# Group sums of the first image by TensorE, fewer loads, and layer 1's weights prepared in the opening

## The chip, the core and the metric

The kernel runs on one core of one Trainium2 chip, in one launch. The metric is the device time of that core in microseconds (us), taken from three runs; a further run was profiled, and the profile is what is read here. The core has TensorE (PE in the profile, its weight loads PEld), VectorE (DVE), ScalarE (ACT), GpSimd (POOL) and SyncE (SP), each with its own queue of instructions that runs in order. SP and ACT also issue the DMA transfers.

## The reference

Eight images of 384 channels and 32 x 32 tokens pass two layers of attention; layer 1 has a feed-forward part too. Cut to what matters here:

```python
x = x + _L0_conv_ref(_gn(x), L0_conv_qkv_w, ..., L0_conv_mlp_b2)
t = _to_tokens(x)
t = t + _L1_attn_ref(_ln_t(t), L1_attn_qkv_w, L1_attn_proj_w, L1_attn_proj_b)
t = t + _L1_ffn_ref(_ln_t(t), ...)

def _gn(v, G=32, eps=1e-5):                       # 32 groups of 12 channels
    g = v.reshape(B_, G, C_ // G, H_, W_)
    m = jnp.mean(g, axis=(2, 3, 4), keepdims=True)
    s = jnp.var(g, axis=(2, 3, 4), keepdims=True)
    return ((g - m) / jnp.sqrt(s + eps)).reshape(v.shape)

# in _L0_conv_ref: one bias table for all images, (heads, n, n), added to the scores
hidden = jax.nn.gelu(rel @ mlp_w1 + mlp_b1, approximate=False)
bias = hidden @ mlp_w2 + mlp_b2
return jnp.transpose(bias, (2, 0, 1))

# in _L1_attn_ref: q and k, per head of 64
def _normalize(t):
    mu = t.mean(axis=-1, keepdims=True)
    sd = t.std(axis=-1, keepdims=True, ddof=1)
    return (t - mu) / sd
```

In layer 1, subtracting the token's mean and the head's mean commutes with the projection, so the kernel takes both out of the weights once: from each column of the 384 x 1152 projection matrix its mean over the 384 channels, and from each row of a head's 64 columns their mean (for q and k).

## The kernel before, in words

All arithmetic is in 32-bit floats. Channels lie on the 128 partitions in KC = 3 chunks, tokens run along the free axis in two halves of 512. Layer 0 goes image by image: projections of q and k in pairs of heads (`project_qk`, L467, six groups named pq), of v (`project_v`, L495, four groups), then 32 units of scores and weighting. A unit computes scores for two heads (L521), adds the bias (L532, VectorE), takes the exponential (L536, ScalarE), and weighs v (L552) two units later. Four PSUM buffers of 128 x 1024 (`mm2`) serve everything. Layer 1 follows with the same shape and a feed-forward part behind.

The order on each engine is the order in which the program writes it; there is no planner. Work that is to stand beside other work is put into `later` with a number of steps: `later.step()` is called after each pq group, each v group and each unit, and runs what has come due. So in the first image steps 1 to 6 are the projections, 7 to 10 the v groups, and from 11 on the units.

The opening of the first image (L212 to L680) does this. The image is loaded in three chunks on SP; the raw weights of q and k (1.18 MB) are loaded into the space of `grow`, and `place_weights_qk` copies them on VectorE into the padded layout. Statistics of the channels (L418) are sent to DRAM and back on SP, so that the 12 channels of a group lie on one partition; there they are joined (L432), turned into scale and shift on GpSimd, and sent to DRAM and back again (L440, L444); then the image is normalised (L448).

The bias needs one value per head and relative position: 63 x 63 = 3969 of them (NREL). Positions are held in four row groups of 32 partitions, `hidden` computes the first MLP layer (L350) and Gelu (L355) in two rounds of four calls, and `table_part` the second layer (L370), writing its half of the table to DRAM on SP (L379). From the table, `grow_load` reads 32 parts (8 heads x 4), four DMAs of 117 KB each (L391), and `grow_turn` copies each part, turned, into `grow` (L401 on ScalarE, L403 on VectorE). 20 of the 32 parts are due before or at the first units, one per unit after that. The last twelve go through the space of `oT`. A part of the next head pair is used only some units later.

The other loads of layer 0 (bias of q and k in eight pieces, L311; weights of v, bias of v, output weights in six pieces, bias, L319 to L336) are issued by SP between the group norm and the table. ACT issues the small loads of the MLP (L238 to L246) before its first Gelu. [...]

Layer 1's weights are prepared in the last image of layer 0, by `_Start.stages`: loaded at unit 5, column sums by TensorE against a matrix of ones (L146, named cm) at units 10 and 12, their means subtracted by GpSimd (L158), and the heads' means (L164 to L166) at units 19, 21 and 23.

Of the kernel before, what the change touches and what calls it, by code (L numbers as in the profile page):

```python
# [27 lines left out]
P = 128  # L28
# [92 lines left out]
class _Start:  # L121
# [4 lines left out]
    def __init__(self, tc, ins, x1, shared):  # L126
        self.nc, self.ins, self.x1, self.shared = tc.nc, ins, x1, shared

    def load_weights(self):
        self.wqkv = self.shared.weights("wqkv").rearrange("p (k c) -> p k c", k=KC)  # L130
        self.nc.sync.dma_start(
            self.wqkv, self.ins["L1_attn_qkv_wT"].rearrange("(k p) c -> p k c", p=P)
        )
# [5 lines left out]
    def means(self, temp, at, n):  # L139
        nc = self.nc  # L140
        pm = self.shared.mm2(f"cm{at}")
        for h in range(-(-n // HALF)):
            w = min(HALF, n - h * HALF)
            for k in range(KC):
                cols = slice(at + h * HALF, at + h * HALF + w)
                nc.tensor.matmul(  # L146
                    pm[:, h, :w], self.shared.ones, self.wqkv[:, k, cols],
                    start=(k == 0), stop=(k == KC - 1),
                )
        self.mean = temp(f"cmean{at}")  # L150
        nc.scalar.activation(
            self.mean[:, :n], pm.rearrange("p h q -> p (h q)")[:, :n], AF.Copy, scale=1.0 / C
        )

    def subtract(self, at, n):
        for k in range(KC):
            w = self.wqkv[:, k, at : at + n]
            self.nc.gpsimd.tensor_sub(w, w, self.mean[:, :n])  # L158

    def heads(self, k):  # L160
        nc = self.nc
        w = self.wqkv[:, k, 0 : 2 * C].rearrange("p (h d) -> p h d", d=D1)
        hm = self.shared.pool.tile([P, 2 * H1], F32, tag="hm", name=f"hm{k}")
        nc.vector.tensor_reduce(hm, w, AX.X, ALU.add)  # L164
        nc.gpsimd.tensor_scalar(hm, hm, 1.0 / D1, 1.0, ALU.mult, ALU.mult)
        nc.gpsimd.tensor_sub(w, w, hm.unsqueeze(2).to_broadcast([P, 2 * H1, D1]))  # L166

    def stages(self, temp):

        first, rest = (0, 2 * HALF), (2 * HALF, 3 * C - 2 * HALF)  # L170
        return [
            (5, self.load_weights),
            (6, self.load_image),
            (10, lambda: self.means(temp, *first)),
            (11, lambda: self.subtract(*first)),
            (12, lambda: self.means(temp, *rest)),
            (14, lambda: self.subtract(*rest)),
            (19, lambda: self.heads(0)),
            (21, lambda: self.heads(1)),
            (23, lambda: self.heads(2)),  # L180
        ]


def _layer0(tc, ins, x1, sums, shared, beside):
# [9 lines left out]
    with ExitStack() as ctx:  # L194
# [31 lines left out]
        QT, QN = 32, 2 * HALF  # L226
# [5 lines left out]
        nc.vector.memset(rel, 0.0)  # L232
        nc.vector.memset(w2, 0.0)
        nc.vector.memset(b2, 0.0)
        for g in range(P // QT):
            at = g * QN
            n = min(QN, NREL - at)
            nc.scalar.dma_start(rel[g * QT : g * QT + 2, 0:n], ins["rel"][:, at : at + n])  # L238
            nc.scalar.dma_start(w1[g * QT : g * QT + 2], ins["L0_conv_mlp_w1"])
        with nc.allow_non_contiguous_dma(reason="a bias, once"):  # L240
            nc.scalar.dma_start(b1, ins["L0_conv_mlp_b1"].rearrange("(k p) -> p k", p=HC))
            nc.scalar.dma_start(
                w2[:, :, 0:H0], ins["L0_conv_mlp_w2"].rearrange("(k p) h -> p k h", p=HC)
            )
        for g in range(P // QT):
            nc.scalar.dma_start(b2[g * QT : g * QT + H0], ins["L0_conv_mlp_b2"].unsqueeze(1))  # L246
# [8 lines left out]
        first = load(0)  # L255

# [31 lines left out]

        def place_weights_qk():
            whole = 2 * NF0 * D0  # L290
            for s in range(2):
                nc.vector.tensor_copy(
                    wqk[:, :, s, :, 0:D0],
                    raw[:, :, s, 0:whole].rearrange("p k (h d) -> p k h d", d=D0),
                )
                for j in range(2):
                    at = whole + j * D0
                    nc.vector.tensor_copy(
                        wqk[:, :, s, j::2, D0:S0],
                        raw[:, :, s, at : at + D0].rearrange("p k (c d) -> p k c d", d=FR),  # L300
                    )

        def load_bias_qk():
            with nc.allow_non_contiguous_dma(reason="a bias, once"):
                for j in range(2):
                    for row, n, at, step in (
                        (j * S0, D0, j * D0, 2 * D0),
                        (j * S0 + D0, FR, (2 * NF0 + j) * D0, FR),
                    ):
                        for s in range(2):  # L310
                            nc.sync.dma_start(  # L311
                                bqk[row : row + n, s],
                                bass.AP(
                                    qkv_b.tensor, qkv_b.offset + s * C + at, [[1, n], [step, NF0]]
                                ),
                            )

        def load_weights_v_out():
            nc.sync.dma_start(wv, qkv_w[:, 2 * C : 3 * C].rearrange("(k p) c -> p k c", p=P))  # L319
            nc.sync.dma_start(bv, qkv_b[2 * C : 3 * C].partition_broadcast(P))  # L320
            pw = ins["L0_conv_proj_w"]
            for j in range(2):
                last = (2 * NF0 + j) * D0
                for row, n, at, step in (
                    (j * S0 + SP, D0, j * D0, 2 * D0),
                    (j * S0, FR, last, FR),
                ):
                    nc.sync.dma_start(
                        wp[row : row + n],
                        bass.AP(  # L330
                            pw.tensor, pw.offset + at * C, [[C, n], [step * C, NF0], [1, C]]
                        ),
                    )
                nc.sync.dma_start(wl[j * S0 + SP : (j + 1) * S0], pw[last : last + D0])
            with nc.allow_non_contiguous_dma(reason="a bias, once"):
                nc.sync.dma_start(bp, ins["L0_conv_proj_b"].rearrange("(k p) -> p k", p=P))  # L336
# [5 lines left out]
        def hidden(r):  # L342

            hids = {}
            for k in range(2):
                for a in range(2):
                    ph = mm2(f"ph{r}{k}{a}")
                    for i in range(2):
                        g = 2 * a + i
                        nc.tensor.matmul(  # L350
                            ph[0:HC, i], w1[g * QT : g * QT + 2, ts(k, HC)],
                            rel[g * QT : g * QT + 2, ts(r, HALF)], start=True, stop=True,
                        )
                    hid = etile(f"hid{r}{k}{a}", (HC, 2, HALF))
                    nc.scalar.activation(  # L355
                        hid.rearrange("p i q -> p (i q)"), ph[0:HC].rearrange("p i q -> p (i q)"),
                        AF.Gelu, bias=b1[:, k : k + 1],
                    )
                    hids[k, a] = hid
            return hids  # L360
# [5 lines left out]
        def table_part(r, hids):  # L366
            pb = mm2(f"pb{r}")
            for k in range(2):
                for g in range(P // QT):
                    nc.tensor.matmul(  # L370
                        pb[ts(g, QT), 0], w2[:, k, :], hids[k, g // 2][:, g % 2],
# [4 lines left out]
            for g in range(P // QT):  # L376
                at = g * QN + r * HALF
                n = min(HALF, NREL - at)
# [26 lines left out]
        def group_norm(b, xn):  # L405
# [48 lines left out]
            ]  # L454

# [184 lines left out]
        stages = group_norm(0, first)  # L640
        for stage in stages[:3]:
            stage()
        place_weights_qk()
        hids = [hidden(r) for r in range(2)]
        stages[3]()
        load_bias_qk()
        stages[4](nc.vector)
        load_weights_v_out()
        table_part(0, hids[0])
        later.after(1, lambda: table_part(1, hids[1]))  # L650
        nc.scalar.activation(tiny[:, 1:2], tiny[:, 0:1], AF.Exp)
# [14 lines left out]
        for i, n in enumerate((3, 3, 3, 3, 2, 2, 2, 2)):  # L666
            later.after(i + 3 + (i > 3), lambda n=n: grow_turns(n))
            later.after(i + 2, lambda n=n: grow_loads(n))
        for i in range(len(parts) - 20):
# [4 lines left out]
        with_last = beside(etile)  # L674
        for b in range(B):
            held = []
            for i, u in enumerate(units):
# [10 lines left out]
                if b == B - 1:  # L688
                    for at, work in with_last:
# [1085 lines left out]
def tile_conv_attn_hybrid(ctx: ExitStack, tc: tile.TileContext, ins, out):  # L1775
    dram = ctx.enter_context(tc.tile_pool(name="x1", bufs=1, space=DRAM))
    x1 = dram.tile([B, C, N], F32, tag="x1", name="x1")
    state = ctx.enter_context(tc.tile_pool(name="state", bufs=1))
    flag = state.tile([P, 1], mybir.dt.int32, tag="flag", name="flag")
    sums = state.tile([P, B, NP0, 2 * N // P], F32, tag="sums", name="sums")  # L1780
    with ExitStack() as main, tc.manual_schedule():
        shared = _Shared(tc, main)
        start = _Start(tc, ins, x1, shared)
        before = _layer0(tc, ins, x1, sums, shared, start.stages)
# [6 lines left out]
    with tc.If(out_of_range > 0):  # L1791
        _layer0_shifted(tc, ins, x1)
        with ExitStack() as again, tc.manual_schedule():
            shared = _Shared(tc, again)
            start = _Start(tc, ins, x1, shared)
            late = again.enter_context(tc.tile_pool(name="late", bufs=2))
            for _, stage in start.stages(
                lambda name: late.tile([P, N], F32, tag="t", name=name)
            ):
                stage()  # L1800
# [45 lines left out]
```

## Time and profile before

| | us |
|---|---|
| median of three runs (lowest, highest) | 3058.92 (3056.34, 3061.76) |
| the profiled execution, its own time | 3058.54 |
| its span, first to last instruction | 3056.7 |
| TensorE busy in the span | 3023.9 |
| VectorE, ScalarE, GpSimd busy | 1771.8, 1401.7, 463.0 |
| first TensorE matmul | 7.13 |
| first projection of layer 0 | 23.94 |
| first scores of layer 0 | 74.45 |
| first projection of the second image | 189.96 |
| first projection of layer 1 | 1440.39 |

The mean granted clock of TensorE is 0.998 of full. A row of the timeline or of the chain gives the start in us from the span's start, the duration in us, the engine, the line and what it writes and reads; "x16" is a count. TensorE's 32-bit matmuls appear as two records each, so a projection group of 6 matmuls is 12 records. A window's row gives busy time by engine, then the granted clock, the busy share of the 16 DMA engines and GB/s. The share of busy time is high for TensorE everywhere except in the first 100 us, where windows and timeline tell more than the page.

### The profile page before, as it was taken

How to read it: one execution, taken by the hardware profiler on the slowest of the kernel's cores; microseconds unless marked ns; L12 is line 12 of the kernel's file. 1: busy time of each engine (PE TensorE's matmuls, PEld its weight loads, DVE VectorE, ACT ScalarE, POOL GpSimd, SP SyncE). 2: the span in 40 equal slices, each digit the busy share in tenths (PEclk: the TensorE clock that was granted, in tenths of full speed). 3: DMA queues.
4: the chain of work that ended last, by engine and by line, in shares of the span. 5: the costliest groups of instructions: out<-in, count | busy, mean ns of one | idle time of the engine just before them, and what ended most of it. 6: DMA issues, size and time to landing. Idle time of an engine off the chain costs nothing.

```text
span 3056.7 us, 45678 instructions
## 1 busy us (share of the span) xinstructions
PE 3023.9 (99%) x18914; PEld 1595.5 (52%) x18914; DVE 1771.8 (58%) x1768; ACT 1401.7 (46%) x1768; POOL 463.0 (15%) x315
## 2 busy tenths in 40 slices
PE   8999999999999999999999999999999999999998
PEld 3455546455554646444545645645645645644443
DVE  3746647273655637355565765755765755755545
ACT  2634526252443616244453553553544543554544
POOL 0111102021110202123202202202202202211110
PEclk9999999999999999999999999999999999999999
DMA  7412020211202020222401101101101101102011
GB/s 178 118 26 83 19 82 23 71 30 26 76 22 79 23 85 17 50 74 60 117 23 30 50 23 30 50 23 30 50 22 30 50 22 30 50 16 71 16 51 44
DMA packets 102770, 150.49 MB, mean 49 GB/s; under 512 B 62260, under 2 KB 65828, under 8 KB 101784
## 3 DMA queue, kind: packets, MB, share of 16 engines
q1 hardware_dynamic: 99688, 147.41, 16.8%
q8 instruction: 152, 2.49, 0.3%
q14 instruction: 66, 0.54, 0.1%
q10 hardware_dynamic: 2864, 0.05, 0.1%
HBM read 111.05 MB, written 27.32 MB: 45 GB/s over the span
## 4 chain that ended last, share of the span: by engine, by line
PE 92%; DVE 3%; DMA 2%; ACT 1%; SPq 1%; issue 1%; ACTq 0%; DVEq 0%
PE o L552 15%; PE s L521 15%; PE s L1322 11%; PE o L1371 10%; PE pq L467 8%; PE pq L1178 7%; PE y2p L1572 5%; PE pp L616 4%; PE y1p L1521 4%; PE pp L1435 4%; PE pv L1259 4%; PE pv L495 4%; PE sum L1394 1%; DVE qk L1188 1%; PE hs L1207 1%
## 5 line engine op out<-in xcount | busy, mean ns | idle before, releaser
L536 ACT ACTIVATE e<-e 128x1024 f32<-128x1024 f32 x512 | 534.9, 1056 | 441.9 <-DVE e L532 425.3
L532 DVE TENSOR_TENSOR e<-s,grow 128x1024 f32<-128x1024 f32 x512 | 601.0, 1217 | 190.6 <-PE s L521 190.1
L521 PE MATMUL s<-qk 48*64 48x512 f32 x4096 | 605.8, 591 | 2.3 <-DVE e L532 2.2
L552 PE MATMUL o<-e,v 64*64 64x512 f32 x4096 | 603.4, 591 | 1.5 <-DVE e L532 1.5
L1333 ACT ACTIVATE e<-s,kc 128x512 f32<-128x512 f32 x768 | 463.3, 693 | 181.2 <-PE s L1322 164.5
L1322 PE MATMUL s<-qk,qk 64*64 64x512 f32 x3072 | 398.6, 592 | 0.6 <-DVE oT L1381 0.4
L1371 PE MATMUL o<-e,v 64*64 64x512 f32 x3072 | 395.5, 591 | 0.0
L521 PEld LDWEIGHTS s<-qk 48*64 48x64 f32 x4096 | 238.5, 132 | 226.6 <-issue 82.3
L552 PEld LDWEIGHTS o<-e,v 64*64 64x64 f32 x4096 | 257.9, 133 | 182.6 <-issue 80.9
L1348 DVE TENSOR_TENSOR t<-t,e 128x1024 f32<-128x1024 f32 x192 | 230.8, 1221 | 65.6 <-ACT e L1333 65.6
L1178 PE MATMUL pq<-bx,wqkv 128*128 128x512 f32 x576 | 255.4, 596 | 0.7 <-ACT tra L1150 0.7
L467 PE MATMUL pq<-xn,w 128*128 128x512 f32 x576 | 251.5, 597 | 0.0
L1322 PEld LDWEIGHTS s<-qk,qk 64*64 64x64 f32 x3072 | 148.7, 132 | 195.0 <-issue 116.2
L581 POOL TENSOR_TENSOR inv<-sums,over 128x16 f32<-128x16 f32 x32 | 92.7, 2898 | 1015.1 <-DMA sums<-sd 856.0
L1371 PEld LDWEIGHTS o<-e,v 64*64 64x64 f32 x3072 | 148.1, 133 | 180.7 <-issue 142.7
L467 PEld LDWEIGHTS pq<-xn,w 128*128 128x128 f32 x576 | 109.5, 191 | 142.7 <-issue 140.2
L1178 PEld LDWEIGHTS pq<-bx,wqkv 128*128 128x128 f32 x576 | 107.4, 190 | 145.3 <-issue 141.5
L1345 DVE TENSOR_TENSOR t<-e,e 128x1024 f32<-128x1024 f32 x96 | 114.1, 1224 | 62.7 <-ACT e L1333 62.7
L1194 ACT ACTIVATE qsq<-pq 128x1024 f32<-128x1024 f32 x48 | 49.1, 1023 | 215.4 <-DVE qk L1188 110.0
L1508 DVE TENSOR_REDUCE parts<-y 128x1 f32<-128x1024 f32 x75 | 90.0, 1217 | 94.9 <-ACT y L1505 94.4
L1228 POOL TENSOR_TENSOR hc<-hc,rsqrt 128x32 f32<-128x32 f32 x24 | 139.4, 5810 | 2.0
L477 DVE TENSOR_SCALAR qk<-pq,bqk 128x1024 f32<-128x1024 f32 x24 | 30.8, 1284 | 177.6 <-PE pq L467 177.6
(161 smaller groups left out, 3028.3 us busy)
## 6 DMA issues: line engine op xcount, KB each, us to landing
rb<-rd SPq DMA_DIRECT2D x112, 256.0 KB
xn<-in_x_dram SPq DMA_DIRECT2D x24, 512.0 KB
res<-in_x_dram SPq DMA_DIRECT2D x24, 512.0 KB
x<-res SPq DMA_DIRECT2D x24, 512.0 KB
bx<-x SPq DMA_DIRECT2D x8, 1536.0 KB
rq<-hi SPq DMA_DIRECT2D x48, 256.0 KB
out_dram<-bx SPq DMA_DIRECT2D x24, 512.0 KB
wide<-table SPq DMA_DIRECT2D x80, 114.2 KB
```

What stands on the lines that cost most here:

```text
L467: nc.tensor.matmul(pq[:, h], wqk[:, k, s, 2 * pair : 2 * pair + 2, :].rearrange("p h d -> p (h d)"), xn[:, k, ts(h, HALF)], start=(k == 0) ...
L521: nc.tensor.matmul(s[j][ts(c, QP), i], qk[pair][rows, 1, ts(4 * m2 + 2 * i + c, QP)], qk[pair][rows, 0, ts(h, HALF)], start=True, stop=True,)
L532: nc.vector.tensor_add(e.rearrange("p (i q) -> p i q", i=2), s[j], bass.AP(near.tensor, near.offset, [near.ap[0], [-QROWS * IW, 2], [1, HA ...
L536: nc.scalar.activation(e, e, AF.Exp)
L552: nc.tensor.matmul(po[ts(j, S0), r], v[keys, 2 * m2 + i, 2 * pair + j, :], es[j][keys, ts(i, HALF)], start=(m2 == 0 and i == 0), stop=(m2 ...
L1178: nc.tensor.matmul(pq[:, h], wqkv[:, k, s * C + pair * P : s * C + (pair + 1) * P], xt[:, k, ts(h, HALF)], start=(k == 0), stop=(k == KC - 1),
L1228: nc.gpsimd.tensor_tensor(c, c, rsqrt.to_broadcast(list(c.shape)), ALU.pow)
L1322: nc.tensor.matmul(s[j][ts(c, QP), i], qk[pair, 1][rows, ts(4 * m2 + 2 * i + c, QP)], qk[pair, 0][rows, ts(h, HALF)], start=True, stop=True,)
L1333: nc.scalar.activation(e[:, ts(i, HALF)], s[j][:, i], AF.Exp, scale=kc[:, pair, j, m : m + 1])
L1348: nc.vector.tensor_add(total[j], total[j], e)
L1371: nc.tensor.matmul(po[ts(j, D1), r], v[keys, 2 * m2 + i, at : at + D1], es[j][keys, ts(i, HALF)], start=(m2 == 0 and i == 0), stop=(m2 == ...
L1572: nc.tensor.matmul(py[m][:, h], w2[:, k, ts(m, P)], supply.parts[k][i][:, ts(h, HALF)], start=(k == 0 and i == 0), stop=(k == FC - 1 and i ...
```

## The change: what it does

Group norm of the first image. `first_group_norm` keeps mean and variance per channel on its partition (`bn_aggr`), sums them over a group with a matmul against a 0/1 matrix `member`, and spreads the result back with `members`. Both matrices are made on GpSimd by affine selection in a free part of `grow`. The other seven images keep the way over DRAM.

The MLP's loads: positions in two DMAs (of four rows each) and w1 in two, instead of eight; the positions are shared out as 982 + 982 + 982 + 1023 over the row groups (QN and QL), so the zero filling is one column. b1, w2 and b2 move to SP. A dummy Gelu is put ahead so that ScalarE's table is loaded early. `hidden` is called eight times, interleaved with the group norm's steps, and both table parts come before the projections.

The loads of q's and k's bias, of v's weights and bias and of the output weights move from SP to ACT, behind the table parts; layer 1's weights are loaded behind them, also on ACT, into a free part of `grow` (heads 6 and 7). Their column sums come at step 2, between the second and the third projection, the mean at step 3 (now on VectorE), subtractions at steps 4 to 6, heads at 7 to 9, and at step 10 the finished weights are stored to DRAM (`ready`) on SP. In the last image they are loaded from there. Table loads and turns come one step earlier than before.

```diff
-class _Start:
-    def load_weights(self):
-        self.wqkv = self.shared.weights("wqkv").rearrange("p (k c) -> p k c", k=KC)
-        self.nc.sync.dma_start(
-            self.wqkv, self.ins["L1_attn_qkv_wT"].rearrange("(k p) c -> p k c", p=P)
+class _Weights:
+    def load(self, here, mean):
+        self.w = here.rearrange("p (k c) -> p k c", k=KC)
+        self.mean = mean
+        self.nc.scalar.dma_start(
+            self.w, self.ins["L1_attn_qkv_wT"].rearrange("(k p) c -> p k c", p=P)
         )
...
+    def take(self):
+        for at, n, pm in self.sums:
+            self.nc.vector.tensor_scalar_mul(self.mean[:, at : at + n], pm[:, :n], 1.0 / C)
+    def subtract(self, k):
+        self.nc.gpsimd.tensor_sub(self.w[:, k], self.w[:, k], self.mean)
...
-        return [
-            (5, self.load_weights),
-            (6, self.load_image),
-            (10, lambda: self.means(temp, *first)),
-            (11, lambda: self.subtract(*first)),
-            (12, lambda: self.means(temp, *rest)),
-            (14, lambda: self.subtract(*rest)),
-            (19, lambda: self.heads(0)),
-            (21, lambda: self.heads(1)),
-            (23, lambda: self.heads(2)),
-        ]
+    def store(self):
+        self.nc.sync.dma_start(self.ready, self.w.rearrange("p k c -> p (k c)"))
...
-        for g in range(P // QT):
-            at = g * QN
-            n = min(QN, NREL - at)
-            nc.scalar.dma_start(rel[g * QT : g * QT + 2, 0:n], ins["rel"][:, at : at + n])
-            nc.scalar.dma_start(w1[g * QT : g * QT + 2], ins["L0_conv_mlp_w1"])
+        for r in range(2):
+            src = ins["rel"]
             nc.scalar.dma_start(
+                rel[r:P:QT, 0:QL], bass.AP(src.tensor, src.offset + r * NREL, [[QN, P // QT], [1, QL]])
             )
...
+            def means():
+                nc.vector.tensor_scalar_mul(mean, sums(0, mv[:, :, 0]), 1.0 / PG)
+                p = spread(0, mean, 1)
+                nc.vector.tensor_sub(d, mv[:, :, 0], p)
+                nc.vector.tensor_mul(d, d, d)
+                nc.vector.tensor_add(d, d, mv[:, :, 1])
...
-        stages = group_norm(0, first)
-        for stage in stages[:3]:
-            stage()
-        place_weights_qk()
-        hids = [hidden(r) for r in range(2)]
-        stages[3]()
-        load_bias_qk()
-        stages[4](nc.vector)
-        load_weights_v_out()
-        table_part(0, hids[0])
-        later.after(1, lambda: table_part(1, hids[1]))
-        nc.scalar.activation(tiny[:, 1:2], tiny[:, 0:1], AF.Exp)
+        nc.scalar.activation(tiny[:, 1:2], tiny[:, 0:1], AF.Gelu)
+        measure, means, deviations, scales, apply = first_group_norm(first)
+        for n in range(3):
+            hidden(n)
+        measure()
+        means()
+        hidden(3)
+        hidden(4)
+        deviations()
+        place_weights_qk()
+        hidden(5)
+        hidden(6)
+        scales()
+        hidden(7)
+        apply()
+        for r in range(2):
+            table_part(r)
+        nc.scalar.activation(tiny[:, 1:2], tiny[:, 0:1], AF.Exp)
+        load_bias_qk()
+        load_weights_v_out()
+        weights.load(*early)
+        later.after(2, weights.means)
+        later.after(3, weights.take)
+        for i in range(KC):
+            later.after(i + 4, lambda i=i: weights.subtract(i))
+            later.after(i + 7, lambda i=i: weights.heads(i))
+        later.after(KC + 7, weights.store)
...
-            later.after(i + 3 + (i > 3), lambda n=n: grow_turns(n))
-            later.after(i + 2, lambda n=n: grow_loads(n))
+            later.after(i + 2 + (i > 3), lambda n=n: grow_turns(n))
+            if i == 0:
+                grow_loads(n)
+            else:
+                later.after(i, lambda n=n: grow_loads(n))
```

The second path of the program, which starts over when a softmax sum leaves the range of the floats, reads the prepared weights too; it does not run here.

## Prediction

> **What bounds the kernel now.** I read the page first, then the chain in order of time, then the opening's timeline and windows.
>
> ```profile
> PE 3023.9 (99%) x18914; PEld 1595.5 (52%) x18914; DVE 1771.8 (58%) x1768; ACT 1401.7 (46%) x1768; POOL 463.0 (15%) x315
> ```
>
> TensorE is busy almost throughout, so a change pays in two ways: less TensorE work in the dense part, or fewer lost microseconds before it. The chain shows both.
>
> ```profile
> 15.41 5.03 PE ph L350 x16
> 20.44 3.57 PE pb L370 x16
> 24.01 7.23 PE pq L467 x12
> ...
> 33.09 5.36 PE pq L467 x12
> ...
> 76.32 5.42 DMA oT<-table
> 81.76 2.67 DMA wide<-table
> ...
> 85.78 3.62 PE o L552 x16
> 89.40 2.07 PE s L521 x16
> ...
> 1338.59 5.35 PE cm L146 x12
> ...
> 1350.97 0.86 PE cm L146 x6
> ```
>
> The first projection takes 7.23 us where a later one takes 5.2, so TensorE starts at half speed. Scores begin at 74.45 (timeline) but wait for table pieces. A score and a weighting take 1.72 each in the steady chain (91.46 to 93.18 to 94.90); three scores and one weighting come before 89.40, so the opening is worth a start of scores at 89.40 - 6.88 = **82.5**. In the last image "cm", the column sums of layer 1's weights, stands on the chain. Image 6 takes 174.45 us from its first projection to image 7's (1062.21 to 1236.66); in image 7 the same stretch ends at 1417.5 (1415.79 + 1.72), 180.85 us.
>
> ```profile
> 14.25 8.12 ACT L355 ACTIVATE hid<-ph,b 96x1024 f32<-96x1024 f32 x8
> 17.29 3.79 SPq L311 DMA_DIRECT2D bqk<-in_L_conv_qkv_b_dram  x8
> 35.61 4.49 SPq L391 DMA_DIRECT2D wide<-table  x10
> 83.00:84.00 1.00, 1.00 (x6) 0.00 (x0) 0.15 (x1) 0.00 (x0) 0.00 (x0) 0.50 0.92 241
> ```
>
> Gelu starts at 14.25 because ScalarE first issues 14 loads. Table reading starts at 35.61. The last row, a window, shows the clock (0.50) after a gap of 2.22 us at 78.1: it was low from 82.7 to 89.2.
>
> [...] The trace can't show a big ACT load beside SP's (all big ones are SP's); its DMA share is 1.05 from 70 to 74, so nothing is free for a second stream then.
>
> **The change, part by part.**
>
> *Last image.* cm, three pairs of subtractions and three head corrections go. TensorE loses 180.85 - 174.45 = **6.4 us** of chain. The GpSimd and VectorE work was hidden behind scores: nothing. The prepared weights are loaded at the same step with the same bytes: nothing.
>
> *Group norm through TensorE.* Before: statistics end at 9.24, four small transfers (18 and 3 KB) pass, normalisation runs 18.80 to 21.06. After: three bn_aggr, 12 one-or-two-column matmuls and five tiny vector steps, about 0.1 to 0.2 each with their handovers, and 0.57 + 0.25 on GpSimd (the rows of before). They are interleaved with "hidden", whose Gelus set the pace, so normalisation runs about 15.3 to 17.6. TensorE needs it only after the table matmuls, so this wait leaves the path.
>
> *Fewer loads.* ACT issues 4 loads instead of 14. b1 stands fourth on SP behind three image loads; the third has landed at 7.95, so I put b1 at 9.0 (8.4 to 10). Eight Gelus take 8.12: **17.1**. The Exp table load and its dummy (1.28 + 0.20) end at 18.6. Eight Gelus share four PSUM buffers, so the first table matmuls start when the sixth is done, 15.2 against 20.37 before. Both table parts now stand ahead of the projections: 2 x 3.6 cold = 22.4, second part out at 23.2 (0.75). Table reading can begin at 25 instead of 35.6.
>
> *Loads moved from SP to ACT.* [...] From 18.6, ACT issues eight bqk (3.79): 22.4; then wv, bv, wp, wl, bp. Without waits these took 4.5 on SP (21.13 to 25.61): 26.9. But in the changed program bv waits for a table write, the wp and wl pieces for table writes or one another, bp for a table read, and layer 1's weights for a wp piece. With 2.2 us for a small write (9.26 to 11.44 before) and 3 to 4 for 0.1 to 0.6 MB, their load (1.77 MB) is issued at **31** (27 to 33). Queued behind on ACT: eviction of projection 0,1 and ACT's table turns. [...]
>
> *Arrival.* 3 to 9 us moved 334 to 408 GB/s, so 1.77 MB needs 4.7 and about 2.2 fixed: 38 alone. [...] 38 to 42; I take **40.5**.
>
> *cm moved into the opening.* It stands behind the second projection, so all later TensorE work waits for that load. TensorE arrives at 22.4 + 7.23 + 5.16 = 34.8 and stands until 40.5: a **new wait of 5.7**. It costs 6.2 itself (5.35 + 0.86). The clock falls: [...] I take 2.6. Four projections: 20.6. The fifth projection now reuses the buffer of the fourth, which ACT must evict first (1.11 and handovers): 1.3. Four v groups: 15.6. Scores start at 40.5 + 6.2 + 2.6 + 20.6 + 1.3 + 15.6 = **86.8**.
>
> *Table feed.* After the weights, 16.5 parts at 1.95 (before, the turns of three parts begin at 60.62, 62.47 and 64.52) and six qk copies (0.77 MB, 3.3) bring the twentieth part at about 40.5 + 2 + 32.2 + 3.3 = 78.0, ahead of 86.8: the waits at 78 to 89 go. They are the 8.1 inside 82.5.
>
> *Moved small work.* Subtracting (3 x 2.6, scaled from 7.02 for three 1024-wide), heads (3 x 1.7) on GpSimd and 4.3 us on VectorE lie under projections of 3.9 to 5.2 us each; if this cover fails, the store is late. The store (1.77 MB on SP) waits for the last head correction, about when scores start; parts 22 and 23 queue behind it and land within a microsecond of their need. Nothing to 3 us; I take nothing.
>
> Sum: (86.8 - 82.5) - 6.4 = **-2.1**. The profiled execution took 3058.54 (span 3056.7): 3056.4. The median of the runs is 0.38 higher: **3056.8**.
>
> Unknown costs: group masks by affine selection have no row. Lower bound: hidden (they can start at 4.9 and are wanted at 8.6, when ACT's dummy Gelu, behind them, should have run). Upper: per column a scalar operation takes 1.2 ns there (1197 ns for 1024) and a power 169 (5.41 us for 32); 10 lies between, and four selections of 960 columns in all take 9.7: end 14.6. I take hidden. A shift moves everything equally.
>
> **Rivals.**
> *A, the weights arrive in time* (35 or before): ACT's waits are shorter and the reads yield. Scores start at 34.8 + 6.2 + 20.6 + 1.3 + 15.6 = 78.5, the feed keeps up (35 + 37.5 = 72.5), sum -10.4: **3048.5**. For: 26.9 + 7 = 34 without waits. Against: the waits named.
> *B, slower, masks on GpSimd:* ACT's first Gelu and the group sums wait for four selections. Each us past 9.0 costs one; no gain is left when they end after 11.1. At 14.6 the shift is 5.6: **3062.4**. For: a power of 32 columns takes 5.4 there. Against: plain arithmetic is fast.
> *C, the feed still rules:* by bytes, 20 parts, copies, layer 0's loads and layer 1's weights are 13.0 MB, 55.4 us at 235 GB/s after 27: 82.4, hidden below 86.8. But the store adds 7.5 us at that rate before part 22; with 3 of it exposed and 2 for the clock: **3061.8**.
> That the change doesn't do what it says is excluded for cm: it is absent from the last image's order.
>
> **How the numbers follow.** 0.2% (6.1 us) is about what a measurement tells from no change. Likeliest 0.50: arrival 37 to 44 [...], from -6.5 to +2.0, nearly all within. A 0.26, faster. B 0.11 and C 0.13, about a third over the bound. Faster 0.30, same 0.57, slower 0.13. The likeliest alone: 3052 to 3061; with A and the ends of B and C: 3048 to 3065.
>
> **What would show it.** Gelus from about 9; pb's 32 records in a row from about 15; normalised image before 18; a TensorE gap of some 6 us ahead of cm, ended by the load of layer 1's weights; clock 0.5 after it; no waits for table pieces after scores start near 87; last image 174.5. Wrong, if that gap is missing (A), Gelus start after 11 (B), or scores wait after 85 for parts behind the store (C).

## The result, and the profile after

| | before | changed |
|---|---|---|
| median of 8 runs (lowest, highest) | 3059.22 (3056.34, 3061.76) | 3068.18 (3065.95, 3068.87) |
| profiled execution, its own time (span) | 3058.54 (3056.7) | 3065.95 (3064.0) |
| first scores of layer 0 | 74.45 | 93.55 |
| first projection of the second image | 189.89 | 202.36 |
| first projection of the last image | 1236.59 | 1249.11 |
| first projection of layer 1 | 1440.39 | 1445.94 |

The starts are read from the timeline; the chain, which the prediction used, has such groups about 0.07 later (93.62 for the scores below). The ratio is 1.0032 (95% interval 1.0023 to 1.0041): slower by 9.0 us, where 2.1 us faster was forecast. The profiled run is the fastest of the changed kernel's eight, so the profiles differ by only 7.3 us of span. Taken apart by the starts of the images: the opening lost 12.47 (202.36 - 189.89); the last image with what follows up to layer 1 won 6.97 (196.83 instead of 203.80 from its first projection to layer 1's first); layer 1's first image lost 0.57 (173.18 instead of 172.61), which no run took apart; the tail lost 1.2. Its last matmuls took 7.11 us instead of 5.42 (the granted clock of the changed kernel is 0.67 from 3048 to 3050 and 0.50 from 3050 to 3052, where they begin, and 1.00 in these matmuls of the kernel before), of which more below.

The chain in order of time, of the changed kernel (start, duration, engine or DMA, what):

```profile
20.31 3.64 PE pb L400 x16
...
32.63 5.64 DMA wp<-in_L_conv_proj_w_dram
...
38.30 9.84 DMA grow<-in_L_attn_qkv_wT_dram
48.14 0.14 issue
48.27 7.80 PE cm L145 x18
56.07 10.31 PE pq L559 x24
...
66.41 1.12 ACT qk L573
...
67.57 10.57 PE pq L559 x24
78.14 15.48 PE pv L587 x48
93.62 5.91 PE s L613 x45
```

And TensorE's waits in the first 110 us (total, times, longest):

```profile
PE cm L145 <- DMA grow<-in_L_attn_qkv_wT_dram: 11.8, 1, 11.8
...
PE pq L559 <- ACT qk L573: 1.2, 1, 1.2
```

The new wait at cm is there, where it was forecast, but 11.8 us long instead of 5.7. TensorE stands idle for that time; this is called the stand below. The load of layer 1's weights was issued at 38.30 and landed at 48.14. The 1.2 before the fifth projection (forecast 1.3) is the PSUM buffer that ACT had to evict. ACT's timeline tells why the load was late:

```profile
10.04 3.11 ACT L386 ACTIVATE hid<-ph,b 96x1024 f32<-96x1024 f32 x3 [2.35 <-PE ph L381]
14.94 2.11 ACT L386 ACTIVATE hid<-ph,b 96x1024 f32<-96x1024 f32 x2 [1.79 <-PE ph L381]
18.12 3.35 ACT L386 ACTIVATE hid<-ph,b 96x1024 f32<-96x1024 f32 x3 [1.07 <-PE ph L381]
...
29.52 0.36 ACTq L351 DMA_DIRECT2D bv<-in_L_conv_qkv_b_dram  x1
...
32.63 2.55 ACTq L359 DMA_DIRECT2D wp<-in_L_conv_proj_w_dram  x2
...
38.30 0.39 ACTq L132 DMA_DIRECT2D grow<-in_L_attn_qkv_wT_dram  x1
```

Two things. ScalarE waits for "ph" ahead of the first Gelu, which starts at 10.04 instead of 9.0, and twice more between the Gelus (1.79 and 1.07 us), so the last ends at 21.47 instead of 17.1. And of the loads ahead of layer 1's, bv is issued at 29.52, though wv ahead of it was out by 25.3; a table write had landed at 29.31. The last pieces of wp and wl are out by 36.2, bp at 37.03, and layer 1's weights at 38.30, when a piece of wp had landed at 38.28 (the chain). The windows of the stand (busy time by engine, granted clock, DMA share, GB/s):

```profile
36.00:44.00 8.00, 0.46 (x2) 0.00 (x0) 0.00 (x0) 1.59 (x2) 0.00 (x0) 0.85 0.99 274
44.00:52.00 8.00, 3.73 (x5) 1.71 (x6) 0.65 (x1) 0.59 (x1) 0.00 (x0) 0.51 0.91 221
```

The granted clock falls in the stand (0.51 from 44 to 52) and cm takes 7.80 instead of 6.2. The DMA engines are 0.91 to 1.09 busy in the windows of 8 us from 36 to 92: the load of 1.77 MB, with table reads beside it, took 9.84 us. ACT's load and SP's table reads, under way together, kept the engines 0.99 busy at 274 GB/s from 36 to 44.

The load also held up the reads in another way, which the prediction did not price. SP's waits in the first 110 us have this line:

```profile
SPq L421 <- DMA grow<-in_L_attn_qkv_wT_dram: 5.5, 1, 5.5
```

After fourteen table reads SP issued none from 42.6 to 48.1, and the fifteenth went out at 48.15, when the load had landed (48.14). The engines were busy meanwhile (0.98 and more in the windows of 40 to 48), so the records don't tell what of the slow reads is due to the load under way beside them and what to the pause in SP's issues, and no run below separates the two.

### The profile page after: what moved, and what is told of

The parts are those of the page before. It is cut to its first block, busy times and chain, and to the rows that moved or that the text cites. A ratio compares the mean times of both kernels' runs of the same rounds, so it can differ in the third digit from the quotient of the medians.

```text
span 3064.0 us, 45736 instructions
## 1 busy us (share of the span) xinstructions
PE 3022.1 (99%) x18938; PEld 1591.5 (52%) x18938; DVE 1772.7 (58%) x1778; ACT 1400.9 (46%) x1767; POOL 465.3 (15%) x316
## 3 DMA queue, kind: packets, MB, share of 16 engines
q1 hardware_dynamic: 96744, 147.61, 17.2%
## 4 chain that ended last, share of the span: by engine, by line
PE 93%; DVE 3%; DMA 1%; ACT 1%; issue 1%; ACTq 0%; SPq 0%; DVEq 0%
PE s L613 15%; PE o L644 14%; PE s L1431 11%; PE o L1480 11%; PE pq L559 8%; PE pq L1287 7%; PE y2p L1681 5%; PE pp L708 4%; PE y1p L1630 4%; PE pv L587 4%; PE pp L1544 4%; PE pv L1368 4%; PE sum L1503 1%; DVE qk L1297 1%; PE hs L1316 1%
## 5 line engine op out<-in xcount | busy, mean ns | idle before, releaser
L624 DVE TENSOR_TENSOR e<-s,grow 128x1024 f32<-128x1024 f32 x512 | 601.4, 1219 | 185.9 <-PE s L613 184.4
L1303 ACT ACTIVATE qsq<-pq 128x1024 f32<-128x1024 f32 x48 | 49.1, 1023 | 216.1 <-DVE qk L1297 110.3
```

The costliest lines, as they stand in the source:

```text
L624: nc.vector.tensor_add(e.rearrange("p (i q) -> p i q", i=2), s[j], bass.AP(near.tensor, near.offset, [near.ap[0], [-QROWS * IW, 2], [1, HA ...
```

## The experiments

Each was timed in five rounds beside the kernel before (whose medians lay between 3057.6 and 3058.3, some 1 to 1.6 below the 3059.22 of the table above). "Opening" is the first projection of the second image, 189.89 before and 202.36 in the changed kernel.

| run | median (lowest, highest) | ratio to before, 95% | opening |
|---|---|---|---|
| e1_sums_late | 3063.92 (3061.08, 3066.44) | 1.0018 (1.0011, 1.0025) | 199.69 |
| e2_weights_ahead | 3060.18 (3058.18, 3062.25) | 1.0005 (0.9997, 1.0013) | 196.90 |
| e3_weights_first | 3057.11 (3055.49, 3058.85) | 0.9996 (0.9988, 1.0004) | 193.43 |
| e4_no_prep | 3062.32 (3059.29, 3064.83) | 1.0013 (1.0006, 1.0020) | 194.64 |
| e5_no_prep_turns | 3059.61 (3057.11, 3060.85) | 1.0004 (0.9995, 1.0012) | 191.45 |
| e6_loads_early | 3049.94 (3049.25, 3050.80) | 0.9973 (0.9963, 0.9984) | 188.49 |
| e7_gn_dram | 3051.53 (3049.34, 3052.93) | 0.9979 (0.9971, 0.9988) | 191.06 |
| e8_others_early | 3050.19 (3048.92, 3052.24) | 0.9974 (0.9965, 0.9983) | 190.19 |
| e9_warm | 3047.92 (3047.04, 3048.68) | 0.9967 (0.9955, 0.9979) | 186.13 |
| e10_kept_warm | 3060.53 (3058.66, 3061.91) | 1.0005 (0.9997, 1.0014) | 198.74 |
| e11_full_array | 3060.95 (3059.65, 3064.30) | 1.0009 (1.0003, 1.0016) | 201.96 |

### Was it the stand alone? e1, e2, e3

e1_sums_late puts the column sums and what follows them later:

```diff
-        later.after(2, weights.means)
-        later.after(3, weights.take)
+        later.after(5, weights.means)
+        later.after(6, weights.take)
...
-            later.after(i + 4, lambda i=i: weights.subtract(i))
-            later.after(i + 7, lambda i=i: weights.heads(i))
-        later.after(KC + 7, weights.store)
+            later.after(i + 6, lambda i=i: weights.subtract(i))
+            later.after(i + 8, lambda i=i: weights.heads(i))
+        later.after(KC + 8, weights.store)
```

e2_weights_ahead changes the order on ACT:

```diff
+        weights.load(*early)
         load_weights_v_out()
-        weights.load(*early)
```

e3_weights_first issues the load on SP, as soon as its place in `grow` is named:

```diff
-        self.nc.scalar.dma_start(
+        self.nc.sync.dma_start(
             self.w, self.ins["L1_attn_qkv_wT"].rearrange("(k p) c -> p k c", p=P)
...
         early = late[:, GW * IW : GW * IW + KC * 3 * C], late[:, 0 : 3 * C]
+        weights.load(*early)
...
         load_weights_v_out()
-        weights.load(*early)
```

> The column sums stand behind the fifth projection instead of the second (their mean, the subtractions, heads and the store follow; nothing else differs from the changed kernel). Theory Wait (the loss is TensorE standing 11.8 us for layer 1's weights, and 1.6 us of half clock behind it): the stand goes, scores start near 80, time 3068.2 - 13.4 = 3055. Theory Feed (the table reads, with 3 MB of other loads now among them, could not have fed the scores before about 88 anyway; the stand only hid that): scores start near 80 but wait for table pieces up to about 88 to 90, time 3061 to 3064, and the waits of before for table pieces are back.

> The load of layer 1's weights is issued on ACT ahead of the loads of v's and the output weights instead of behind them; same bytes. Theory Wait: it is issued near 25 instead of 38.3, lands near 34 to 36, TensorE hardly stands at the sums (0 to 1 us), time near 3055. Theory Feed: the bytes in the stretch are the same, so the start of scores moves from 93.6 only to about 88 to 90, time 3061 to 3064; the stand turns up again ahead of v (its weights late) or as waits for table pieces.

> The load of layer 1's weights is issued on SP right behind the raw weights of q and k and the small MLP loads, in the first 10 us, before any table read. Both theories expect no stand at the sums. Theory Wait: scores start near 80, time 3055. Theory Feed: 1.8 MB less in the stretch of the table reads is worth 7 to 8 us of it, the twentieth part comes near 82, time 3051 to 3055. Against both: the load slows the image and the raw weights in the first 15 us, Gelus or the normalised image come up to 4.7 us later: 3056 to 3059.

None of the three has the stand any more, and cm takes 5.8 to 6.0. Had the stand been all, each would have come to 3055. By the medians e1 won 4.3 of the 13.4 us, e2 8.0, e3 11.1; by the openings it is 2.7, 5.5 and 8.9, as the kernel before also ran 1 to 1.6 faster here than beside the changed kernel. So the amounts are good to some 2 us, their order is not in doubt. In e1 TensorE now waits at the scores (and 3.69 us in v, where ACT is behind). TensorE's and VectorE's timeline of e1:

```profile
71.61 13.27 PE L587 MATMUL pv<-w,xn 128*128 128x384 f32 x36 [3.69 <-ACT qk L573]
84.81 4.16 PE L613 MATMUL s<-qk 48*64 48x512 f32 x32
92.36 3.96 PE L613 MATMUL s<-qk 48*64 48x512 f32 x13 [3.39 <-DVE e L624]
```

```profile
90.52 0.65 DVE L433 COPY grow<-wide 128x480 f32<-128x480 f32 x1 [2.78 <-DMA wide<-table]
91.09 4.60 DVE L624 TENSOR_TENSOR e<-s,grow 128x1024 f32<-128x1024 f32 x4
```

Its first addition of the bias (e, L624) starts at 91.09, right behind the turn of the twentieth table piece at 90.52; in e2 that turn is at 88.44, in e3 at 84.95. So the feed of the table was a second bound, a little below the first, and the stand only hid it. The earlier the 1.77 MB leave the stretch of the table reads, the earlier that piece comes. Theory Feed holds for e1, and for e2 but for 1 us. e3 is 2 us slower than both theories allow: the twentieth piece comes at 84.95, not near 82, and its projections start at 27.17 instead of 25.89. In part that is its "pb" (6.6 us; 5.7 in the changed kernel, but 6.7 and 6.6 in e1 and e2 too, so the difference is no mark of e3). Its time lies in the range that the expectation had "against both", but not for the reason given there: the Gelus start only 0.4 later, at 10.43.

### What else is in the opening: e4, e5

e4_no_prep has the class `_Start` and its stages in the last image as before, and in `_layer0`:

```diff
-        weights.load(*early)
-        later.after(2, weights.means)
-        later.after(3, weights.take)
...
-        later.after(KC + 7, weights.store)
...
+        with_last = beside(etile)
```

e5_no_prep_turns is e4 and

```diff
-            later.after(i + 2 + (i > 3), lambda n=n: grow_turns(n))
+            later.after(i + 3 + (i > 3), lambda n=n: grow_turns(n))
```

> Layer 1's weights are prepared in the last image as in the kernel before; group norm by TensorE, the fewer loads and the loads on ACT stay as changed. Theory Wait: no stand, no sums in the opening, scores could start near 73, the last image costs its 7.0 us again: 3048 to 3052. Theory Feed: table reads from 30.4 without layer 1's weights, 11.3 MB at 225 GB/s, give the twentieth part near 81, against 82.5 before: 3056 to 3059, with waits for table pieces as before.

> The kernel without the early preparation (3062.3), and in it the turns of the first twenty table pieces one step later, as in the kernel before. Theory Turns (with the earlier turns the first addition of the bias stands on VectorE behind the turn of the twentieth piece, which its unit doesn't need; before, the first unit ran ahead of it): one unit of 3.4 us is won in the opening, 4 at most: 3058 to 3059. Theory Feed alone (the pieces come at the same time, so nothing moves): 3062. Pieces land at the same times in both.

e4 met neither theory. Without layer 1's weights the opening is still 4.75 us longer than before (194.64), although table reading begins at 30.24 instead of 35.61. The twentieth piece is turned at 85.23 (before, at 83.85): the 5.4 us of the earlier start are more than used up. That v's and the output weights, now loaded among the reads, use them up is argued here; e6 and e8 below bear it out. And the units start later for the same feed. VectorE's timeline of the kernel before, of e4 and of e5:

```profile
83.85 0.65 DVE L403 COPY grow<-wide 128x480 f32<-128x480 f32 x1 [2.42 <-DMA wide<-table]
84.42 2.34 DVE L532 TENSOR_TENSOR e<-s,grow 128x1024 f32<-128x1024 f32 x2
```

```profile
85.23 0.65 DVE L431 COPY grow<-wide 128x480 f32<-128x480 f32 x1 [2.93 <-DMA wide<-table]
85.80 4.60 DVE L622 TENSOR_TENSOR e<-s,grow 128x1024 f32<-128x1024 f32 x4
```

```profile
80.15 0.65 DVE L431 COPY grow<-wide 128x480 f32<-128x480 f32 x1 [2.79 <-DMA wide<-table]
80.72 2.35 DVE L622 TENSOR_TENSOR e<-s,grow 128x1024 f32<-128x1024 f32 x2
85.30 0.65 DVE L431 COPY grow<-wide 128x480 f32<-128x480 f32 x1 [2.23 <-DMA wide<-table]
85.87 2.35 DVE L622 TENSOR_TENSOR e<-s,grow 128x1024 f32<-128x1024 f32 x2
```

In e4 all four additions stand behind the turn at 85.23. In e5, with the turns one step later as before, the first unit runs at 80.72, and its opening is 3.2 us shorter (time 2.7). This is theory Turns, which forecast 3.4; the time is 0.6 above its range. The earlier turns are a part of the change that my sum left out altogether. With it undone, and no early preparation, the rest of the change comes out even with before (1.0004).

### The other loads: e6, e8

e6_loads_early is e3, and in `load_bias_qk` and `load_weights_v_out` every `nc.scalar` becomes `nc.sync`, and both are called early:

```diff
-            nc.scalar.dma_start(wv, qkv_w[:, 2 * C : 3 * C].rearrange("(k p) c -> p k c", p=P))
+            nc.sync.dma_start(wv, qkv_w[:, 2 * C : 3 * C].rearrange("(k p) c -> p k c", p=P))
...
+        load_bias_qk()
+        load_weights_v_out()
         oT = kept.tile([P, NP0, N], F32, tag="oT", name="oT")
...
-        load_bias_qk()
-        load_weights_v_out()
```

e8_others_early is the changed kernel with this edit alone; `weights.load` stays where it was, on ACT.

> The kernel with layer 1's weights loaded first (3057.1), and in it the loads of q's and k's bias and of v's and the output weights also on SP in the first 20 us, behind layer 1's weights, instead of on ACT behind the Gelus. Theory Feed (these 1.2 MB ran among the table reads at 200 to 235 GB/s, about 5 us[...]): reads begin near 28.5 instead of 30.8, the twentieth piece comes near 77 instead of 85, TensorE's own path (v ends near 81) becomes the bound, 5 us won: 3052. Theory Reads (the table reads are limited by themselves, by their buffers or their issue): at most the 2 to 3 us of the earlier start: 3054 to 3055.

> The changed kernel, in which only the loads of q's and k's bias and of v's and the output weights go out on SP in the first 20 us; the load of layer 1's weights keeps its place on ACT behind the Gelus. Theory Queue (the load was late because ACT issued it behind these 16 others[...]): it is issued near 23 instead of 38.3, with only table writes beside it, lands at 30 to 33, before TensorE arrives at 36.5; no stand, the table reads run among it and 1.2 MB less: 3050 to 3053. Theory Place (a load behind the Gelus is too late wherever the others are): it lands after 38, TensorE stands 2 us or more at half clock, 3055 or more.

Both are faster than either kernel of the study, by 8 and 7.4 us than before. e8 answers the question of the stand: one load in the place where the change put it, but without the 17 others in front (eight pieces of bqk, wv, bv, six of wp and wl, bp). ACT's timeline and the windows of e8:

```profile
18.97 3.35 ACT L388 ACTIVATE hid<-ph,b 96x1024 f32<-96x1024 f32 x3 [1.07 <-PE ph L383]
21.22 0.41 ACTq L132 DMA_DIRECT2D grow<-in_L_attn_qkv_wT_dram  x1
22.34 1.28 ACT L751 ACT_TABLE_LOAD   x1
```

```profile
20.00:24.00 4.00, 4.00 (x21) 0.83 (x21) 2.42 (x4) 3.68 (x5) 0.00 (x0) 1.00 0.88 179
24.00:28.00 4.00, 4.00 (x21) 0.89 (x14) 0.97 (x2) 0.00 (x0) 0.00 (x0) 1.00 0.90 357
28.00:32.00 4.00, 4.00 (x11) 1.78 (x10) 0.53 (x1) 0.00 (x0) 0.00 (x0) 1.00 0.31 78
```

It is issued at 21.22 and the burst of 357 GB/s is over by about 29, some nine us ahead of cm (37.94), which waits for nothing. The time is the one of theory Queue; theory Place is out. The other loads (1.2 MB, half of it wv) fill the time up to 20; from 8 on the DMA engines of the changed kernel were 0.23 busy there (0.59 in e8). Now the table reads run undisturbed. The queue of SP, in the changed kernel and in e6:

```profile
24.76 5.51 SPq L409 DMA_DIRECT2D table<-part  x8
30.44 27.76 SPq L421 DMA_DIRECT2D wide<-table  x36
```

```profile
24.92 3.77 SPq L412 DMA_DIRECT2D table<-part  x8
28.88 17.20 SPq L424 DMA_DIRECT2D wide<-table  x36
```

36 reads are issued within 17.2 us instead of 27.8, the eight table writes within 3.77 instead of 5.51. In e6 the twentieth piece is turned at 80.74, right behind v's last addition; TensorE reaches the scores at 79.69 without a wait, and its own path is the bound. Theory Feed came out 2 us too slow here, Reads is out.

### The group norm and the clock: e7, e9, e10, e11

e7_gn_dram is e6 with the group norm of before:

```diff
-        measure, means, deviations, scales, apply = first_group_norm(first)
...
+        stages = group_norm(0, first)
+        for stage in stages[:3]:
+            stage()
+        load_weights_v_out()
         place_weights_qk()
+        for n in range(8):
+            hidden(n)
+        stages[3]()
+        weights.load(*early)
+        load_bias_qk()
+        stages[4](nc.vector)
```

e9_warm is e6 with 20 matmuls ahead of the group norm's definition:

```diff
+        warm = mm2("warm")
+        for n in range(20):
+            nc.tensor.matmul(
+                warm[:, 0, 0:P], shared.ones, shared.ones, start=True, stop=True
+            )
         measure, means, deviations, scales, apply = first_group_norm(first)
```

e10_kept_warm is e9 with a filler behind each group of `hidden` (filler is a part of v, all ones then):

```diff
+            nc.tensor.matmul(
+                ph[HC:P, 0, 0 : 2 * P], shared.ones[:, 0 : P - HC], filler, start=True, stop=True
+            )
             hid = etile(f"hid{n}", (HC, 2, HALF))
```

e11_full_array is e9 with two fillers ahead of each group:

```diff
             ph = mm2(f"ph{n}")
+            for _ in range(2):
+                nc.tensor.matmul(
+                    ph[:, 0, 0:P], shared.ones, shared.ones, start=True, stop=True
+                )
```

> As the kernel with all loads early on SP, but the first image's group norm by way of DRAM as in the kernel before (layer 1's weights load behind its transfers). Theory Sums-hold-up (the small matmuls of the group sums stand among the first MLP layer's at half clock and keep ScalarE waiting 2.9 us, and the last Gelu ends at 21.5 instead of 18.2): Gelus run 10 to 18.2 without a break, projections start near 22 to 23 instead of 27, 3047 to 3049. Theory Sums-help (the way over DRAM is late again, the normalised image comes after 25 because its transfers stand behind others): 3052 to 3056.

> The kernel with all loads early on SP and group sums by TensorE (3049.9), and in it 20 matmuls of ones with ones ahead of the first MLP layer, whose output nobody reads: extra work for TensorE in its empty first 8 us. Theory Clock (the opening runs at half clock, which holds up the Gelus by 3 us and the table matmuls by 2): ph matmuls take half, Gelus run nearly without a break and end near 18.5 instead of 21.6, projections start near 22 instead of 25.8: 3045.5 to 3047. Theory Handover (the Gelus wait for the group sums' way between engines, not for the clock): 3049 to 3051.

> The kernel with the 20 idle matmuls at the start (3047.9), and in it one further matmul of 256 columns (ones with ones, 0.43 us at full clock) behind each of the eight groups of the first MLP layer, into 32 unused partitions of its PSUM tile; nobody reads its output. Theory Share (the clock falls to 0.50 from 12 to 20 because TensorE has gaps between the Gelus, short as they are): with the gaps filled it stays full, the table matmuls take 3.7 to 4 us instead of 6.1, projections start near 21 instead of 23.5: 3045 to 3046. Theory Ration (the clock falls at that place whatever TensorE does): the further matmuls run at half clock too and hold the Gelus up, 3048 to 3051.

> As the run with a further matmul at each of the eight groups of the first MLP layer, but with two of 128 x 128 by 128 columns (ones with ones, 0.43 us together at full clock) ahead of each group instead of one of 128 x 32 by 256 behind it; their output is overwritten. Theory Array (what keeps the clock is not that TensorE is busy but how much of its array works: ph matmuls use 2 rows of 128, the further ones of the last run 32 columns): the clock stays at 1.00 for most of 8 to 20, the last Gelu ends before 19, projections start by 22: 3045 to 3047. Theory Ration (the clock falls there whatever TensorE does): it is 0.50 from 12 on again and the extra work costs 3 us or more: 3051 to 3061.

e7 landed between its theories. ScalarE's and TensorE's timeline:

```profile
10.25 8.12 ACT L386 ACTIVATE hid<-ph,b 96x1024 f32<-96x1024 f32 x8 [2.56 <-PE ph L381]
```

```profile
8.19 8.25 PE L381 MATMUL ph<-rel,w 2*96 2x512 f32 x32 [8.19 <-DMA w<-in_L_conv_mlp_w_dram]
16.37 6.05 PE L400 MATMUL pb<-hid,w 96*32 96x512 f32 x32
25.35 13.60 PE L559 MATMUL pq<-xn,w 128*128 128x512 f32 x24 [2.93 <-DVE xn L478]
```

Without the group sums the eight Gelus run in 8.12, so it is these sums that hold them up by 3.3. But the image is normalised only at 26.65 (its transfers share the queue with the loads), TensorE waits 2.93 for it, and its first two projections (24 records) then take 13.6 instead of 10.6. Group sums by TensorE are worth 1.6 us net in this setting (2.6 in the opening), with the order of loads that the way over DRAM needs: it differs from that of e6 too.

e9 showed the slow pace at the start to be a cost of its own: with TensorE busy from 1 us on, the first twelve records of "ph" take half the time (1.96 us instead of 3.73), the last Gelu ends at 18.70 instead of 21.64, and projections start at 23.48 instead of 25.82. Theory Clock was missed by 1 us; it is the fastest kernel of the study, 9.7 us ahead of before (ratio 0.9967). But the gain stops there, since the clock falls at 12, to 0.52 and 0.50 (windows of e9):

```profile
8.00:12.00 4.00, 3.57 (x32) 1.92 (x32) 1.57 (x7) 2.76 (x3) 0.00 (x0) 1.00 1.01 339
12.00:16.00 4.00, 4.00 (x25) 2.22 (x23) 2.16 (x8) 3.25 (x4) 1.28 (x2) 0.52 0.93 334
16.00:20.00 4.00, 4.00 (x19) 1.00 (x18) 2.42 (x4) 3.61 (x4) 0.00 (x0) 0.50 0.50 146
```

e10 and e11 were to hold it and failed, e11 against the explanation formed after e10. (The 0.43 us of their expectations is an estimate, half of the 0.86 that 512 columns take, a sixth of a projection's 5.16.) e10 came to 3060.5, some 9 above theory Ration too: the fillers, at a clock of 0.50 themselves from 12 on, hold the Gelus up, and the last of them starts at 30.60 instead of 17.59. e11 lies in the range of theory Ration, its last Gelu starts at 33.55. Windows of e10:

```profile
16.00:20.00 4.00, 4.00 (x12) 0.78 (x7) 0.48 (x3) 1.11 (x1) 0.00 (x0) 0.50 0.07 12
...
28.00:32.00 4.00, 4.00 (x20) 1.21 (x20) 2.42 (x4) 1.69 (x3) 0.00 (x0) 0.50 0.00 0
```

TensorE is busy for 4.00 of 4.00 us in each window from 16 to 32 (3.54 from 12 to 16) and still at 0.50, as far as modelled ends of matmuls tell, through "ph" matmuls of 2 x 96 and fillers of 128 x 32. e11 has two fillers of the whole 128 x 128 array for each "ph" group (1.22 of every 3.1 us) and stays at 0.50 from 12 to 36. In e9, e10 and e11 the clock came back during the "pb" that follow (0.66 to 0.74 in their windows). So neither a TensorE busy for 4.00 of 4.00 us (e10) nor fillers of the whole array for a share of 0.39 (e11) kept the clock at 1.00; what would, no run shows.

## Why the prediction was wrong

**Last image, right:** 6.97 won, 6.4 forecast. The work moved out of it stayed under TensorE's in the opening, as forecast.

**Group norm and Gelus, wrong in part.** Masks by affine selection ended at 7.40, so rival B is out, and they cost nothing. But the step "their Gelus set the pace" failed. The group sums stand between "ph" groups on TensorE, at the slow pace of the start ("ph" at 3.73 us for twelve records, 1.96 in e9), and hold ScalarE up: Gelus took 11.4 from 10.04, not 8.12 from 9.0. The image was normalised from 19.51 to 21.77 instead of 15.3 to 17.6, still ahead of need. "pb" began at 20.24 instead of 15.2, five us late, and yet TensorE came to cm at 36.46, only 1.7 after the forecast 34.8. That was luck: two prices erred the other way, "pb" took 5.7 instead of 7.2 and the first two projections 10.57 instead of 12.4.

**Issue of the weights, the step that failed.** 31 was taken, 27 to 33 allowed; it was 38.30. Of the 7.3 by which it came late, 2.4 are the late Gelus (the eight bqk were issued by 24.85, not 22.4). The other 4.9 are the waits behind that: 13.4 us from there to the load, where 8.6 were priced. I had found these waits, but charged a small write 2.2 us and a piece of wp 3 to 4, a price that no row of before shows. In company with wv and the table reads two writes took 3.90 and 2.64 and the piece 5.64 (the chain), and they stand in series. The flight of 9.5 us, an estimate (4.7 for the bytes, 2.2 fixed, the rest for table reads beside it), was right (9.84), and so the stand came out as 11.81: 7.3 later issue, 0.3 longer flight, less 1.7 by which TensorE came later too, make 5.9 of the 6.1 over the 5.7. Clock and cm (7.80, forecast 8.8, of which 2.6 for the clock was an estimate, below the 3.2 that 6.5 us at half clock, as from 82.7 to 89.2 before, would cost; 1.6 was measured), PSUM wait (1.20, 1.3), projections and v (20.9 and 15.5) were right within 1 us: 93.62 against 86.8 is the weights' 7.6, less 0.8. Another 1.3 goes between the first scores and the second image (108.8 us, where the prediction's sum implies 107.4); e6, e8 and e9 have the same 108.8 without a stand, and no run isolates its cause.

**Table feed, wrong, and hidden.** The twentieth piece was put at 78.0 from "1.95 a part"; e1 and e2 have it at 90.5 and 88.4. The estimate by bytes in rival C (82.4) was nearer and still short, as the rate from 60 to 76 was 203 GB/s in the changed kernel and 213 in e1 instead of 235, and reading began at 30.4 instead of 25 to 27. It made no difference to the time because the stand was longer, but rival A fell by it: in e2 the weights came in time, and it ran 3060.2, not 3048.5. That number was reached (e8, 3050.2) only when the other loads left the stretch too.

**Turns one step earlier, not priced.** Worth 2.7 where the feed binds (e4 to e5). In the changed kernel, too, such a turn (at 94.60) stands ahead of the first addition (95.61); what it costs there no run shows. **Store, right:** issued at 93.54, and no later piece waited for; rival C's exposed store did not come.

**The rest:** 0.57 in layer 1 and 1.2 in the tail, on no list of mine, and 1.9 more by which the changed kernel's profiled run lay below its median. Opening + 8.2, last image - 0.6, these + 1.8 and + 1.9: 11.3 of the 11.4 between 3056.8 and 3068.18. The range was too narrow because it took the ends of the arrival (37 to 44) from a chain of waits each priced as if without company (its 2.2 for a write is from 9.26 to 11.44 of the kernel before, where the DMA engines were 0.33 busy).

## What to carry to other kernels

Before a load is moved to another queue, follow every issue ahead of it to the landing it waits for, and price those landings with the traffic of the new place, not of the old: here 1.2 MB in 17 loads went ahead of a 1.8 MB load, behind two writes and a piece of wp that took 3.90, 2.64 and 5.64 us to land, and putting these other loads into a stretch in which the DMA engines had been 0.23 busy (e8) made a loss of 9 us a gain of 7. When a wait looks like the whole loss, compute the next bound under it before promising its removal (e1 gave back a third at most). Where an engine works in the order of the program, as VectorE does here, due times of work that is not urgent are part of the path: one step earlier put the first addition at 85.80 instead of 80.72 and cost 2.7 us (e4 to e5).

## What was not expected of the hardware

The tail has a pause of TensorE ahead of its last 12 records. In the 13 profiles, one of each kernel, it is 2.03 to 2.56 us long, and these records then take either 5.42 (5 times) or 7.11 (8 times), without regard to its length: 2.54 gave 5.42, 2.09 gave 7.11. TensorE's timeline of e1 and of e5:

```profile
3045.70 5.42 PE L1544 MATMUL pp<-oT,L_attn_proj_wT 128*128 128x512 f32 x12 [2.54 <-DVE oT L1528]
```

```profile
3043.34 7.11 PE L1536 MATMUL pp<-oT,L_attn_proj_wT 128*128 128x512 f32 x12 [2.09 <-DVE oT L1520]
```

In the changed kernel, with a pause of 2.55, the granted clock is 0.67 and 0.50 in the two windows in which they begin (3048 to 3050 and 3050 to 3052); in the kernel before, with a pause of 2.20, it is 1.00. What decides between the two no run shows. So up to 1.7 us between two profiles can come from this alone; as each kernel has one profile, no run shows how it varies within one kernel. Nor do the runs show what the clock follows: in e10 it is 0.50 for the 20 us from 12 to 32, in which TensorE is busy all but 0.46 us, and in the kernel before it was 0.50 from 82.7 to 89.2 after a pause of 2.22 us. And the record has the clock at 1.00 from the start on, though matmuls run at about half speed at first (before: 3.64 for the first 16 records of "pb" and 1.92 for the other 16, 7.23 for the first projection and 5.36 for the second, with 1.00 in all windows from 20 to 32; in e9 "ph" takes half as long under the same 1.00), so its 1.00 can't be relied on there.
